# Products 2 and 4 of the query projection in a second level of Strassen's form, four query buffers and a new order of the cycle

## The chip, the cores and the metric

The kernel runs on one core of a Trainium2 chip. A core has TensorE (matmuls; results go to PSUM), VectorE, ScalarE and GpSimd (element-wise work) and SyncE, which here issues the DMAs. Each engine works through its own instruction queue in order, and waits on semaphores for the others. The metric is the device time of one execution in microseconds.

## The reference, cut to what matters

64 sequences of 128 tokens, 512 wide. All is in float32.

```python
def ref(x, attn_bias, mask, g_in, null_attn_bias, null_kv, Wq, Wkv, Wo, g_out):
    xn = layernorm(x, g_in)                       # (64, 128, 512)
    q = (xn @ Wq).reshape(b, n, 16, 64).transpose(0, 2, 1, 3) * 64 ** -0.5
    k, v = split(xn @ Wkv)                        # one head of 64 for all 16
    k, v = with_null_row(k, v, null_kv)
    sim = einsum('bhid,bjd->bhij', q, k) + bias   # bias: null column, attn_bias
    sim = where(causal and mask, sim, -max)
    out = einsum('bhij,bjd->bhid', softmax(sim), v)
    out = out.transpose(0, 2, 1, 3).reshape(b, n, 1024) @ Wo
    return x + layernorm(out, g_out)
```

## The kernel before

The sequences go in 16 groups `g` of four (`GB`). The 512 x 1024 query weight `wq` and a group's transposed tokens `xT[g]` (512 x 512) are cut into two by two blocks, and the query projection is one level of Strassen's form in Winograd's order: seven products instead of eight. `weight_sum` and `token_sum` make the sums (weights once, on VectorE; tokens four times per group, on GpSimd, tiles `xS`). `product` (L496) is, for one of four column blocks f, two matmuls with a stationary tile of 128 x 128 and 256 moving columns. Products 1, 6 and 7 gather in one PSUM tile `pa`, 5 and 3 in `pc`, product 2 is in `pw`; `keep` copies a state of `pa` on ScalarE, `q_out` adds it to another on VectorE and writes it into the query tile `qT`, which has two buffers of a whole group. The output projection has the same form for pairs of sequences (`out_product`, L758, `out_sum` on GpSimd).

The order of the steady part is written by hand, in `cycle(c)` for c = 1 to 29. A cycle carries two sequences through each stage: softmax of b0 = 2c and b1 = 2c+1 (`scores_max`, `exps`, `rinv`, `scale`, `blocks_T`), output projection of the pair from p = b0-2, norm and store of r = b0-4 and r+1, tokens of m = b0+10 and m+1 loaded and normalised, query products for f = 0, 1 (c even) or 2, 3 (c odd) of group (2c+4)//4, key and value products of sequences b0+6 and b0+7 (`key_values`: `kv_mm` L358 on TensorE, `kv_out` L373 on VectorE). It ends with `region(c)`: scores of sequences 2c+2 and 2c+3 (L551), then the values of b0 and b1 (L668).

Tokens are transposed on VectorE in blocks (`tokens_T`, L330) and go through memory: at the end of an even cycle `tokens_out` (L339) stores a finished group from `xb` to `xd`, next to `keys_send` (kb on VectorE L399, then kd L404) and `values_send` (L385). The odd cycle after it begins on SyncE with two loads of x (L127), four fetches of keys (L413), four of values (L391), a mask (L144) and the four fetches of `tokens_in` (L347), which fill `xT` of the group whose first sequence is b0+6. The stores of finished sequences (L839) and the loads for the residual (L137) follow in the same queue.

In `cycle` before, the key/value products come late: product 6 of the second half, then

```python
        key_values(b0 + 6)
        q_one(c, 7, 1)
        key_values(b0 + 7)
```

and after them `out_one(p, 3)`, products 3 and 4, `out_one(p, 4)` and `region(c)`. The token sums stand at the end of the odd cycles, behind `region`.

Of the kernel before, what the change touches and what calls it, by code (L numbers as in the profile page):

```python
# [17 lines left out]
def kernel(  # L18
# [63 lines left out]
    P = 128  # L82
# [347 lines left out]
    def q_tile(g):  # L430
        qT[g] = gp.tile([P, NF, GB, NQ, 2, Q], FP, tag="qT", name=f"qT_{g}")

    def q_part(g, c, lo=0, hi=GB):

        return qT[g][:, c % NF, lo:hi, :, c // NF, :]

    def q_half(c, h):
        if c == 0 and h == 0:
            q_tile(0)
        pq = (ps_y if h else ps_q).tile(  # L440
            [P, HT], FP, tag="XY"[c % 2] if h else "ac"[c % 2], name=f"pq_{c}_{h}"
        )
        two = slice(2 * h, 2 * h + 2)
        for kc in (2, 0, 3, 1):
# [8 lines left out]
            q_part(0, c, two.start, two.stop),  # L453
            pq.rearrange("p (t i q) -> p t i q", t=2, i=NQ),
        )

# [9 lines left out]
    def token_sum(g, k):  # L466
# [11 lines left out]
        nc.gpsimd.tensor_tensor(xS[g, k], p, m, ALU.subtract)  # L478

# [29 lines left out]
    def q_out(g, c, toks, tag, name=None):  # L509
        lo = toks.start // N  # L510
        o = q_part(g, c, lo, lo + 2)
# [33 lines left out]
    def heads(b, hf, to):  # L545
        g, t = divmod(b, GB)
        for f in range(NF):
            for r in range(2):
                rows = slice(r * DH, (r + 1) * DH)
                for i in range(2):  # L550
                    nc.tensor.matmul(  # L551
                        to[r][i * DH : (i + 1) * DH, f, :],
                        qT[g][rows, f, t, NQ - 1 - i if hf else i],
# [217 lines left out]
    def y_half(b, e):  # L771
        if b not in ys:
            if at_end:
                ys[b] = at_end[0][:, b - (B - 6)]
# [77 lines left out]
    def q_one(c, k, h):  # L852
# [82 lines left out]
    def cycle(c):  # L935
# [8 lines left out]
        if not first:  # L944
# [90 lines left out]
        if soft:  # L1035
            exps(b1, 1, 4, 7)
        out_one(p, 7)
        if soft:
            exps(b1, 1, 7)
# [369 lines left out]
```

## Time and profile before

| | |
|---|---|
| median of 3 runs | 1040.6 us (1040.02 to 1041.3) |
| the profiled execution | 1040.6 us |
| its span in the profile | 1038.8 us |
| mean granted TensorE clock | 0.998 |
| instructions | 31012 |

The profile lists for each engine its busy time, for groups of instructions their count and mean duration and the idle time before them with what ended it, the chain of work that ended last (followed back from the end, with the share of each engine), the same chain piece by piece in order of time, and the timeline of each engine. Times in a chain or timeline are start and duration in us from the span's start. A float32 matmul is recorded as two matmul records, so "x4" of a query product are two matmuls, and "x8" of a key/value product four. SPq is SyncE's queue: its rows are the issues of DMAs, not the transfers.

### The profile page before, as it was taken

What the parts mean: (1) busy time and instruction counts of PE and PEld (TensorE: products, weight loads), DVE (VectorE), ACT (ScalarE), POOL (GpSimd) and SP (SyncE); (2) the same over time, 40 slices, a digit from 0 to 9 for tenths busy, and PEclk for the clock granted to TensorE, in tenths of its full rate; (3) what the DMA queues carried; (4) which work ended last, traced back from release to release, by engine and by line L of the source; (5) the groups of instructions that cost most, each with busy time, mean ns of one, the idle gap of its engine ahead of it and who ended that gap; (6) DMA issues with size and microseconds to landing.
All of it is one profiled execution on the core that took longest, in us unless ns stands there. A gap on an engine that the chain in (4) does not pass through costs nothing.

```text
span 1038.8 us, 31012 instructions
## 1 busy us (share of the span) xinstructions
PE 1024.2 (99%) x11856; PEld 896.4 (86%) x11856; DVE 771.2 (74%) x1664; ACT 665.9 (64%) x2799; POOL 711.0 (68%) x530
## 2 busy tenths in 40 slices
PE   8999999999999999999999999999999999999996
PEld 7888888888888888888888888888888888888875
DVE  7776677787677786677776777776786876766688
ACT  2665677565776566776656776657765657765581
POOL 3697767676775857767577676757758587666774
PEclk9999999999999999999999999999999999999999
DMA  6633160432515134151341504334151341502202
GB/s 210 157 121 85 52 182 27 146 92 94 144 52 153 57 120 128 42 169 50 127 112 67 169 25 150 88 103 137 51 154 55 123 125 42 166 12 73 83 11 92
DMA packets 68690, 105.10 MB, mean 101 GB/s; under 512 B 8641, under 2 KB 32833, under 8 KB 66753
## 3 DMA queue, kind: packets, MB, share of 16 engines
q1 hardware_dynamic: 67440, 102.08, 32.3%
q8 instruction: 96, 1.57, 0.7%
q10 hardware_dynamic: 1104, 1.05, 0.3%
q14 instruction: 50, 0.40, 0.1%
HBM read 67.45 MB, written 35.65 MB: 99 GB/s over the span
## 4 chain that ended last, share of the span: by engine, by line
PE 92%; ACT 3%; DVE 3%; DMA 1%; POOL 1%; issue 1%; POOLq 0%; DVEq 0%; ACTq 0%
PE pa L496 20%; PE pyX L758 19%; PE pc L496 10%; PE pyY L758 9%; PE ps L551 9%; PE pkv L358 5%; PE pyw L758 5%; PE pw L496 5%; PE poX L668 4%; PE pq L445 2%; ACT s L599 2%; PE pos L668 2%; PE poY L668 1%; DMA x<-in_x_dram 1%; DVE y_end L821 1%
## 5 line engine op out<-in xcount | busy, mean ns | idle before, releaser
L599 ACT ACTIVATE s<-s,nmax 128x65 f32<-128x65 f32 (+1 forms) x1024 | 377.5, 393 | 0.0
L535 POOL TENSOR_TENSOR s<-biasp,mneg 128x1552 f32<-128x1552 f32 x64 | 206.2, 3223 | 70.6 <-DVE sb L635 58.9
L599 ACT ACTIVATION_READ_ACCUMULATOR s<-s,nmax 128x1 f32 x1024 | 221.3, 216 | 0.0
L620 POOL TENSOR_TENSOR s<-s,rinv 128x1024 f32<-128x1024 f32 (+1 forms) x128 | 190.4, 1488 | 44.5 <-DVE rinv L616 44.5
L635 DVE STREAM_TRANSPOSE sb<-s 128x1536 f32<-128x1536 f32 x64 | 113.5, 1773 | 43.2 <-POOL s L620 43.0
L585 DVE TENSOR_TENSOR s<-ps,s 128x256 f32<-128x256 f32 (+2 forms) x224 | 120.0, 605 | 16.9 <-PE ps L551 14.7
L496 PE MATMUL pa<-xS,wq 128*128 128x256 f32 x480 | 123.4, 379 | 0.5 <-ACT ku L507 0.5
L758 PE MATMUL pyX<-wo,oT 128*128 128x256 f32 x512 | 121.6, 380 | 0.3 <-POOL oT L741 0.3
L741 POOL TENSOR_TENSOR yS<-oT 128x512 f32<-128x512 f32 x32 | 40.9, 1278 | 117.2 <-ACT oT L708 113.0
L708 ACT ACTIVATE oT<-poX,nv 128x256 f32<-128x256 f32 x59 | 28.0, 475 | 143.8 <-PE poX L668 74.4
L590 DVE TENSOR_REDUCE nmax<-s 128x8 f32<-128x520 f32 (+1 forms) x128 | 116.4, 948 | 0.0
L758 PE MATMUL pyX<-wT,oT 128*128 128x256 f32 x488 | 115.4, 379 | 0.3 <-POOL oT L741 0.3
L758 PEld LDWEIGHTS pyX<-wo,oT 128*128 128x128 f32 x512 | 96.8, 190 | 15.3 <-issue 1.3
L758 PEld LDWEIGHTS pyX<-wT,oT 128*128 128x128 f32 x488 | 92.6, 190 | 13.3 <-POOL oT L741 0.7
L496 PEld LDWEIGHTS pa<-xS,wq 128*128 128x128 f32 x480 | 88.9, 190 | 11.7 <-ACT ku L507 0.9
L551 PEld LDWEIGHTS ps<-kT,qT 64*64 64x64 f32 x4096 | 85.6, 134 | 11.5 <-issue 11.4
L551 PE MATMUL ps<-kT,qT 64*64 64x128 f32 (+1 forms) x4096 | 93.7, 245 | 0.6 <-issue 0.6
L517 DVE TENSOR_TENSOR qT<-pc,ku 128x256 f32<-128x256 f32 x120 | 50.4, 420 | 58.6 <-ACT ku L507 43.5
L514 ACT COPY qT<-pa 128x256 f32<-128x256 f32 x60 | 23.0, 383 | 101.7 <-PE pa L496 101.7
L288 POOL TENSOR_TENSOR rstd<-rstd,nhalf 128x1 f32<-128x1 f32 x64 | 35.7, 559 | 66.6 <-DVE rstd L287 66.6
L668 PE MATMUL pos<-sb,vr 32*64 32x128 f32 (+1 forms) x1792 | 81.0, 321 | 0.0
L668 PE MATMUL poY<-sb,vr 32*64 32x128 f32 x720 | 74.4, 347 | 0.0
(113 smaller groups left out, 2299.8 us busy)
## 6 DMA issues: line engine op xcount, KB each, us to landing
x<-in_x_dram SPq DMA_DIRECT2D x64, 256.0 KB, 5.4
res<-in_x_dram SPq DMA_DIRECT2D x64, 256.0 KB, 3.1
out_dram<-y SPq DMA_DIRECT2D x58, 256.0 KB, 2.0
xd<-xb SPq DMA_DIRECT2D x14, 1024.0 KB
xT<-xd SPq DMA_DIRECT2D x56, 256.0 KB, 6.1
vr<-vd SPq DMA_DIRECT2D x64, 128.0 KB, 8.5
kT<-kd SPq DMA_DIRECT2D x64, 64.0 KB, 9.6
kd<-kb SPq DMA_DIRECT2D x16, 128.0 KB
```

Of the source, the lines that this page charges most:

```text
L358: nc.tensor.matmul(pkv, xT[g][:, t, kc, :], wkv[:, kc, :], start=(kc == 0), stop=(kc == KC - 1),)
L496: nc.tensor.matmul(prod[tag], w[:, kc, f * P : (f + 1) * P], t[:, :, kc, :], start=(start and kc == 0), stop=(kc == HK - 1), skip_group_ch ...
L517: nc.vector.tensor_tensor(o, p, k, ALU.add)
L535: nc.gpsimd.tensor_tensor(S[b], biasp, mneg[:, t].unsqueeze(1).broadcast_to([P, R8, ROW]), ALU.add,)
L551: nc.tensor.matmul(to[r][i * DH : (i + 1) * DH, f, :], qT[g][rows, f, t, NQ - 1 - i if hf else i], kT[g][rows, 0 : NQ if hf else NQ // 2, ...
L585: nc.vector.tensor_tensor(sv, ps, sv, ALU.add)
L590: nc.vector.tensor_reduce(nmax[b][:, hf], S[b][:, :, WITH_NULL[hf]], AX.X, ALU.max, negate=True)
L599: nc.scalar.activation(row, row, AF.Exp, bias=nmax[b][:, hf, k : k + 1], accum_out=rsum[b][:, hf, k : k + 1],)
L620: nc.gpsimd.tensor_tensor(sv, sv, rinvs.pop((b, hf)).unsqueeze(2).broadcast_to([P, R8, sv.shape[2]]), ALU.mult,)
L635: nc.vector.transpose(sb.rearrange("p j e q -> p e j q"), S[b][:, :, 1 : ROW - 1].rearrange("p e (j k) -> p e j k", k=Q),)
L668: nc.tensor.matmul(po[s][rows, half], vr[g][quad(s), j, t, :], sb[quad(s), slots, r * NF : (r + 1) * NF, :], start=start, stop=True, skip_ ...
L758: nc.tensor.matmul(prod[key], h[:, c, :], w[:, c, :], start=(start and c == 0), stop=(c == HC - 1), skip_group_check=not start,)
```

## The change

Products 2 (weight block a12) and 4 (a22) get a second level from c = 2 on. Each is cut again into two by two blocks of 128 rows, 128 columns and 128 tokens, for a pair of f at once: `leaf(c, k, stage)` issues seven matmuls of 128 columns in four stages (one, three, two, one), all into three slices of one PSUM tile of `ps_w`, and after each stage VectorE adds slices onto the query tile (`onto`, two additions in stage 1, else one). `leaf_weights` makes the sums of weight blocks on GpSimd, three of them at the end of cycle 1 for each product and one at the start of cycle 2; `leaf_sums` makes those of the tokens, four for each product and group, in even cycles. Where product 2 was added to a kept copy of product 1, product 1 is now copied into the query tile (`first_into`) and the narrow products are added to it there; product 4 is added to a copy of the state behind product 7.

The query tile becomes four tiles by pair of f and pair of sequences, one buffer each, whose places change between even and odd groups; the tile for the last six outputs becomes three tiles in the same places.

The order of `cycle` is new for all cycles: the second half's product 1 and `key_values(b0 + 6)` come before `out_one(p, 6)`, `key_values(b0 + 7)` comes last before `region`, both `bias_add` stand behind the last `scale`, and the token sums stand at the start of the even cycles. The diff, without changes of indices that follow from the tiles and without `q_first`, which nothing calls:

```diff
@@ -427,19 +427,27 @@
     s3 = a21
     xS, prod, kept = {}, {}, {}
-    def q_tile(g):
-        qT[g] = gp.tile([P, NF, GB, NQ, 2, Q], FP, tag="qT", name=f"qT_{g}")
-    def q_part(g, c, lo=0, hi=GB):
-        return qT[g][:, c % NF, lo:hi, :, c // NF, :]
-    def q_half(c, h):
+    GH, FH = GB // 2, NF // 2
+    def q_tile(g, fp):
+        for h in range(2):
+            slot = 2 * fp + h if g % 2 == 0 else fp + 2 * h
+            qT[g, fp, h] = gp.tile(
+                [P, FH, GH, NQ, 2, Q], FP, tag=f"q{slot}", name=f"qT_{g}_{fp}_{h}", bufs=1
+            )
+    def q_part(g, c, h):
+        f = c % NF
+        return qT[g, f // FH, h][:, f % FH, :, :, c // NF, :]
...
             4: (b21, xS.get((g, 2))),
         }[k]
         nc.gpsimd.tensor_tensor(xS[g, k], p, m, ALU.subtract)
+    LEAF = 2
+    wL = const.tile([P, 2, 3, FH, P], FP, name="wL")
+    xL, leaves = {}, {}
+    def by_block(tag):
+        return prod[tag].rearrange("p (t i q) -> p t i q", t=2, i=NQ)
+    def first_into(g, c, h):
+        nc.scalar.copy(q_part(g, c, h), by_block("a"))
+    def leaf_blocks(k):
+        w = (a12 if k == 2 else a22).rearrange("p k (f r m) -> p k r f m", r=2, m=P)
+        return w[:, 0, 0], w[:, 1, 0], w[:, 0, 1], w[:, 1, 1]
+    def leaf_weights(k, j):
+        w11, w12, w21, w22 = leaf_blocks(k)
+        t1, t2, t4 = (wL[:, k // 4, i] for i in range(3))
+        o, p, m, op = {
+            1: (t1, w21, w22, ALU.add),
+            2: (t2, t1, w11, ALU.subtract),
+            4: (t4, w12, t2, ALU.subtract),
+            3: (w21, w11, w21, ALU.subtract),
+        }[j]
+        nc.gpsimd.tensor_tensor(o, p, m, op)
+    def leaf_tokens(g, k):
+        b = xT[g][:, 0:GH, hi_k] if k == 2 else xS[g, 4]
+        return b[:, 0, 0], b[:, 1, 0], b[:, 0, 1], b[:, 1, 1]
+    def leaf_sums(g, k):
+        xL[g, k] = gp.tile([P, 3, N], FP, tag=f"xL{k}", name=f"xL{k}_{g}", bufs=1)
+        b11, b12, b21, b22 = leaf_tokens(g, k)
+        t1, t2, t3 = (xL[g, k][:, i] for i in range(3))
+        for o, p, m in ((t1, b12, b11), (t3, b22, b12), (t2, b22, t1), (b12, b21, t2)):
+            nc.gpsimd.tensor_tensor(o, p, m, ALU.subtract)
+    def leaf(c, k, stage):
+        g, f = divmod(2 * c + 4, GB)
+        if g >= NG:
+            return
+        fp = f // FH
+        if stage == 0:
+            leaves[k] = ps_w.tile([P, 3, N], FP, tag="w", name=f"pl{k}_{g}_{f}")
+        pw, pY, pX = (leaves[k][:, i] for i in range(3))
+        w11, w12, w21, w22 = (w[:, fp] for w in leaf_blocks(k))
+        v1, v2, v4 = (wL[:, k // 4, i, fp] for i in range(3))
+        b11, t4, b21, b22 = leaf_tokens(g, k)
+        t1, t2, t3 = (xL[g, k][:, i] for i in range(3))
+        out = qT[g, fp, 0][:, :, :, :, k // 4, :]
+        def mm(to, w, t, start=False):
+            nc.tensor.matmul(to, w, t, start=start, stop=True, skip_group_check=True)
+        def onto(o, p):
+            nc.vector.tensor_tensor(o, p, o, ALU.add)
+        def one(p):
+            return p.rearrange("p (i q) -> p i q", i=NQ)
+        def two(p):
+            return p.rearrange("p a (i q) -> p a i q", i=NQ)
+        if stage == 0:
+            mm(pX, w11, b11, True)
+            onto(out[:, 0, 0], one(pX))
+        elif stage == 1:
+            mm(pw, w12, b21)
+            mm(pX, v2, t2)
+            mm(pY, v1, t1)
+            onto(out[:, 0], two(leaves[k][:, 0:3:2]))
+            onto(out[:, 1, 1], one(pY))
+        elif stage == 2:
+            mm(pX, w21, t3)
+            mm(pY, v4, b22)
+            onto(out[:, :, 1], two(leaves[k][:, 1:3]))
+        else:
+            mm(pX, w22, t4)
+            onto(out[:, 1, 0], one(pX))
...
@@ -854,11 +970,14 @@
         g, f = divmod(i, GB)
         if g >= NG:
             return
-        if k == 1 and f == 0:
-            q_tile(g)
+        if k == 1 and f % FH == 0:
+            q_tile(g, f // FH)
         if k == 1:
             product(g, f, 1, ps_q, "a")
-            keep("a", "p1")
+            if c >= LEAF:
+                first_into(g, f, 0)
+            else:
+                keep("a", "p1")
         elif k == 2:
             product(g, f, 2, ps_w, "w")
             q_out(g, f, lo_t, "w", "p1")
@@ -869,8 +988,14 @@
             keep("a", "u2")
         elif k == 7:
             product(g, f, 7, ps_q, "a", start=False)
-            keep("a", "u3")
-            q_out(g, HC + f, hi_t, "c", "u3")
+            if c >= LEAF:
+                first_into(g, HC + f, 0)
+                nc.vector.tensor_tensor(
+                    q_part(g, HC + f, 1), by_block("c"), q_part(g, HC + f, 0), ALU.add
+                )
+            else:
+                keep("a", "u3")
+                q_out(g, HC + f, hi_t, "c", "u3")
...
@@ -950,116 +1075,163 @@
                 load_mask(kg + 1)
             if (m - 2) // GB < NG:
                 tokens_in((m - 2) // GB)
+        if c == LEAF:
+            for k in (2, 4):
+                leaf_weights(k, 3)
+        if soft:
+            scores_max(b1, 0)
+        if pair:
+            values_out(p, (0, 2))
+            values_out(p, (1, 3))
         if soft:
             scores_max(b0, 0)
-            scores_max(b0, 1)
-            scores_max(b1, 0)
-        if c % 2 and n0 < B:
-            mask_neg(n0 // GB)
-            if n1 == B - 3:
-                bias_add(B - 2)
+        if first and LEAF <= c and 2 * c + 4 < B:
+            token_sum(c // 2 + 1, 1)
+            token_sum(c // 2 + 1, 2)
+            token_sum(c // 2 + 1, 3)
+        q_one(c, 1, 0)
+        if first and LEAF <= c and 2 * c + 4 < B:
+            token_sum(c // 2 + 1, 4)
+        if fin:
+            pair_stats(r)
+        if first and LEAF <= c and 2 * c + 4 < B:
+            leaf_sums(c // 2 + 1, 2)
         if pair:
-            values_out(p, (0, 2))
             values_out(p + 1, (0, 2))
-        q_one(c, 1, 0)
-        if pair:
-            values_out(p, (1, 3))
             values_out(p + 1, (1, 3))
-            out_sum(p, 0)
-        q_one(c, 2, 0)
+        if soft:
+            exps(b0, 0, 0, 2)
+        if c < LEAF:
+            q_one(c, 2, 0)
+        if fin:
+            pair_stats(r + 1)
+        q_one(c, 5, 0)
         if soft:
             scores_max(b1, 1)
-        q_one(c, 5, 0)
+        if c >= LEAF:
+            leaf(c, 2, 0)
+        q_one(c, 6, 0)
         if soft:
-            exps(b0, 0, 0, 2)
-        q_one(c, 6, 0)
-        if fin:
-            for b in (r, r + 1):
-                pair_stats(b)
-                pair_pow(b)
-        if soft:
-            exps(b0, 0, 2, 7)
+            exps(b0, 0, 2, 8)
+            scores_max(b0, 1)
+        if first and LEAF <= c and 2 * c + 4 < B:
+            leaf_sums(c // 2 + 1, 4)
+        if pair:
+            out_sum(p, 0)
         out_one(p, 1)
+        q_one(c, 7, 0)
+        out_one(p, 2)
         if pair:
             out_sum(p, 1)
         if soft:
-            exps(b0, 0, 7)
+            exps(b0, 1, 0, 6)
+        if fin:
+            pair_pow(r)
+        if soft:
             rinv(b0, 0)
             scale(b0, 0)
-        q_one(c, 7, 0)
-        if pair:
-            out_sum(p, 2)
-        if soft:
-            exps(b0, 1, 0, 6)
-        out_one(p, 2)
-        if pair:
-            out_sum(p, 3)
-        q_one(c, 3, 0)
-        if soft:
-            exps(b0, 1, 6)
-            rinv(b0, 1)
-            scale(b0, 1)
-        q_one(c, 4, 0)
-        if fin:
-            for b in (r, r + 1):
-                pair_nmr(b)
-                pair_norm(b)
-            pair_gain(r)
-            pair_residual(r)
-            store(r)
-        out_one(p, 6)
         if toks:
             norm_stats(m)
             norm_stats(m + 1)
+        if c < LEAF:
+            q_one(c, 4, 0)
+        if pair:
+            out_sum(p, 3)
+        if fin:
+            pair_pow(r + 1)
+        if soft:
+            exps(b0, 1, 6, 8)
+        q_one(c, 3, 0)
+        if soft:
+            rinv(b0, 1)
+        if fin:
+            pair_nmr(r)
+        q_one(c, 1, 1)
+        if c >= LEAF:
+            leaf(c, 2, 1)
+        if fin:
+            pair_norm(r)
+        key_values(b0 + 6)
+        if c % 2 and n0 < B:
+            mask_neg(n0 // GB)
+        if fin:
+            pair_gain(r)
+            pair_residual(r)
         if soft:
             exps(b1, 0, 0, 6)
-            blocks_T(b0)
+            exps(b1, 0, 6, 8)
+            rinv(b1, 0)
+        out_one(p, 6)
+        if fin:
+            pair_nmr(r + 1)
+        if c < LEAF:
+            q_one(c, 2, 1)
+        if pair:
+            out_sum(p, 2)
+        if fin:
+            store(r)
+            pair_norm(r + 1)
+            pair_gain(r + 1)
+        if c >= LEAF:
+            leaf(c, 4, 0)
+            leaf(c, 2, 2)
+        if soft:
+            scale(b0, 1)
+            exps(b1, 1, 0, 4)
+        q_one(c, 6, 1)
+        if n1 == B - 3:
+            bias_add(B - 2)
+        q_one(c, 5, 1)
         out_one(p, 5)
         if soft:
-            exps(b1, 0, 6)
-            rinv(b1, 0)
+            exps(b1, 1, 4, 8)
+        if toks:
+            norm_apply(m)
+        if soft:
+            blocks_T(b0)
             scale(b1, 0)
-        if nxt:
-            bias_add(n0)
+            rinv(b1, 1)
         if fin:
-            pair_gain(r + 1)
             pair_residual(r + 1)
+        out_one(p, 7)
+        q_one(c, 7, 1)
+        if fin:
             store(r + 1)
+        if c >= LEAF:
+            leaf(c, 4, 1)
+        if soft:
+            scale(b1, 1)
+        if c >= LEAF:
+            leaf(c, 2, 3)
+        out_one(p, 4)
         if pair:
             load_res(p)
             load_res(p + 1)
-        q_one(c, 1, 1)
-        if soft:
-            exps(b1, 1, 0, 4)
-        q_one(c, 2, 1)
-        if soft:
-            exps(b1, 1, 4, 7)
-        out_one(p, 7)
-        if soft:
-            exps(b1, 1, 7)
-            rinv(b1, 1)
-            scale(b1, 1)
-        q_one(c, 5, 1)
-        q_one(c, 6, 1)
-        if toks:
-            norm_apply(m)
-            norm_apply(m + 1)
-        key_values(b0 + 6)
-        q_one(c, 7, 1)
-        key_values(b0 + 7)
         if soft:
             blocks_T(b1)
+        if toks:
+            norm_apply(m + 1)
         if nxt:
+            bias_add(n0)
             bias_add(n1)
-        out_one(p, 3)
+        if c >= LEAF:
+            leaf(c, 4, 2)
         q_one(c, 3, 1)
         if toks:
             tokens_T(m)
             tokens_T(m + 1)
-        q_one(c, 4, 1)
+        out_one(p, 3)
+        if c < LEAF:
+            q_one(c, 4, 1)
+        if c >= LEAF:
+            leaf(c, 4, 3)
         if soft:
-            nc.tensor.addr_align(256, offset=183 if c == B // 2 - 3 else 223)
-        out_one(p, 4)
+            nc.tensor.addr_align(256, offset=205 if c == B // 2 - 3 else 223)
+        key_values(b0 + 7)
+        if c == 1:
+            for k in (2, 4):
+                for j in (1, 2, 4):
+                    leaf_weights(k, j)
         if first:
             kg = (b0 + 7) // GB
             if kg < NG:
@@ -1068,9 +1240,7 @@
             if toks:
                 tokens_out(m // GB)
         region(c)
-        if c % 2 and (2 * c + 6) // GB < NG:
-            for k in range(1, 5):
-                token_sum((2 * c + 6) // GB, k)
...
@@ -1225,7 +1395,7 @@
     region(0)
     for c in range(1, B // 2 - 2):
         cycle(c)
-    at_end.append(gp.tile([P, 8, DIM], FP, tag="qT", name="y_end"))
+    at_end.append({})
```

More of the change, by code (lines that the diff above doesn't have):

```diff
@@ L428, with q_half @@
     xS, prod, kept = {}, {}, {}
-    def q_tile(g):
-        qT[g] = gp.tile([P, NF, GB, NQ, 2, Q], FP, tag="qT", name=f"qT_{g}")
-    def q_part(g, c, lo=0, hi=GB):
-        return qT[g][:, c % NF, lo:hi, :, c // NF, :]
-    def q_half(c, h):
+    GH, FH = GB // 2, NF // 2
[8 more added lines that the diff above has]
+        return qT[g, f // FH, h][:, f % FH, :, :, c // NF, :]
+    def q_half(c, h, at=None):
         if c == 0 and h == 0:
[L439 to L442, printed above, removed]
+            for fp in range(2):
+                q_tile(0, fp)
+        tag = at or ("XY"[c % 2] if h else "ac"[c % 2])
+        pq = (ps_q if tag in "ac" else ps_y).tile([P, HT], FP, tag=tag, name=f"pq_{c}_{h}")
         two = slice(2 * h, 2 * h + 2)
@@ L452, in q_half, with q_first @@
         nc.scalar.copy(
-            q_part(0, c, two.start, two.stop),
+            q_part(0, c, h),
             pq.rearrange("p (t i q) -> p t i q", t=2, i=NQ),
         )
+    def q_first(f, k, tag):
+        pool = {"a": ps_q, "c": ps_q, "X": ps_y, "Y": ps_y, "s": ps_s, "w": ps_w}[tag]
+        if f == 0 and k == 1:
+            for fp in range(2):
+                q_tile(0, fp)
+        product(0, f, k, pool, tag, start=k in (1, 2, 5))
+        o = {
+            1: (f, 0),
+            2: (f, 0),
+            6: (f, 1),
+            7: (HC + f, 1),
+            4: (HC + f, 0),
+            5: (HC + f, 1),
+            3: (f, 1),
+        }[k]
+        o = q_part(0, *o)
+        if k in (2, 3, 5):
+            nc.vector.tensor_tensor(o, by_block(tag), o, ALU.add)
+        else:
+            nc.scalar.copy(o, by_block(tag))
     def weight_sum(k):
@@ L509, in q_out @@
     def q_out(g, c, toks, tag, name=None):
-        lo = toks.start // N
-        o = q_part(g, c, lo, lo + 2)
+        o = q_part(g, c, toks.start // HT)
         p = prod[tag].rearrange("p (t i q) -> p t i q", t=2, i=NQ)
@@ L552, in heads @@
                         to[r][i * DH : (i + 1) * DH, f, :],
-                        qT[g][rows, f, t, NQ - 1 - i if hf else i],
+                        qT[g, f // FH, t // GH][
+                            rows, f % FH, t % GH, NQ - 1 - i if hf else i
+                        ],
                         kT[g][rows, 0 : NQ if hf else NQ // 2, t, :],
@@ L773, in y_half @@
             if at_end:
-                ys[b] = at_end[0][:, b - (B - 6)]
+                k = (b - (B - 6)) // 2
+                if k not in at_end[0]:
+                    at_end[0][k] = gp.tile([P, 2, DIM], FP, tag=f"q{k}", name=f"y_end_{k}", bufs=1)
+                ys[b] = at_end[0][k][:, b % 2]
             else:
```

1 line of the change is left out of this document (added).

## The prediction

> **What bounds the kernel now.** I began with the page: shares of each engine, granted clock, chain of work that ended last.
>
> ```profile
> PE 1024.2 (99%) x11856; PEld 896.4 (86%) x11856; DVE 771.2 (74%) x1664; ACT 665.9 (64%) x2799; POOL 711.0 (68%) x530
> PEclk9999999999999999999999999999999999999999
> PE 92%; ACT 3%; DVE 3%; DMA 1%; POOL 1%; issue 1%; POOLq 0%; DVEq 0%; ACTq 0%
> ```
>
> TensorE sets the time: it is on 92% of the chain, at full clock throughout. Any time in which it waits is added to the end, and any matmul time removed is taken off. So I read next the chain inside one cycle of the steady part, from one group of score products (`ps`, the start of `region`) to the next. It is an odd cycle, c = 13.
>
> ```profile
> 504.70 2.84 PE ps L551 x128
> ...
> 510.00 1.06 PE pa L496 x4
> 511.06 0.86 PE pw L496 x4
> ...
> 513.65 1.73 PE pyX L758 x8
> ...
> 528.32 0.89 PE pkv L358 x8
> ...
> 536.15 2.84 PE ps L551 x128
> ```
>
> A cycle is 536.15 - 504.70 = 31.45 us, all of it matmuls. One query product is 0.86 (two matmuls of 256 columns, so 0.43 each), one output product 1.73, one key/value product 0.89 (four matmuls of 128 columns, 0.2225 each). The first query product of a cycle starts 5.30 after the scores, and this cycle's first key/value product 23.62 after them. That product is the first reader of a token group (`xT`) which SyncE fetches in this very cycle; in even cycles the group is there already. SyncE's queue:
>
> ```profile
> 506.72 0.46 SPq L339 DMA_DIRECT2D xd<-xb  x1
> 507.22 1.92 SPq L127 DMA_DIRECT2D x<-in_x_dram  x2
> 511.47 7.79 SPq L391 DMA_DIRECT2D vr<-vd  x4
> 519.84 1.80 SPq L347 DMA_DIRECT2D xT<-xd  x4
> 523.36 5.49 SPq L839 DMA_DIRECT2D out_dram<-y  x2
> ...
> DMA to landing us min/median/max: 4.8/6.1/7.2
> SPq L391 <- DMA x<-in_x_dram: 64.1, 26, 3.0
> ```
>
> The first five rows are in order of time; the sixth is from the view of the tile xT, the seventh from that of SyncE's waits. The tokens go out to memory (`xd`) 2.0 us after the scores began, and the four fetches back (`xT`) are issued only from 519.84, because the fetches of values ahead of them wait for loads of x (64.1 us in 26 waits). The last of the four starts near 519.84 + 1.80 - 0.43 = 521.2 and with the median of 6.1 lands at 527.3, which is 22.6 after the scores. The traffic says the same:
>
> ```profile
> 525.00:527.00 2.00, 2.00 (x11) 1.77 (x10) 1.97 (x4) 2.00 (x12) 0.56 (x1) 1.00 0.91 221
> 527.00:528.20 1.20, 1.20 (x8) 1.04 (x7) 1.17 (x4) 1.20 (x7) 1.01 (x2) 1.00 0.06 21
> ```
>
> The last two columns are the busy share of the DMA engines and GB/s: 221 until 527, 21 after. So the key/value product at 528.32 stands about 1 us behind its data. In another odd cycle even that was too little:
>
> ```profile
> 252.77 2.84 PE ps L551 x128
> ...
> 276.39 0.09 issue
> 276.48 1.13 PE pkv L358 x8
> ...
> 284.55 2.84 PE ps L551 x128
> ```
>
> The product takes 1.13 there instead of 0.89, and the cycle 31.78 instead of 31.45. The fetch is already as late as TensorE can bear.
>
> **The narrow products.** Per cycle from c = 2 on, products 2 and 4 of one f pair, 2 x 4 matmuls of 0.43 = 3.46, become 2 x 7 of 128 columns. The key/value product is the nearest row: same shapes, a new stationary tile for each matmul, 0.2225. 14 x 0.2225 = 3.115. Saved: 0.345 a cycle, over 28 cycles (2 to 29) **-9.7 us**. Bounds: the weight loads are recorded longer than their spacing,
>
> ```profile
> L358 PEld LDWEIGHTS pkv<-wkv,xT 128*128 128x128 f32 x512 | 66.5, 191 | 3.9 <-issue 0.9
> L373 DVE TENSOR_TENSOR kvt<-pkv,nkv 128x128 f32<-128x128 f32 x64 | 18.0, 282 | 3.5 <-PE pkv L358 3.4
> L517 DVE TENSOR_TENSOR qT<-pw,kp 128x256 f32<-128x256 f32 x60 | 25.0, 417 | 2.3 <-PE pw L496 0.3
> L478 POOL TENSOR_TENSOR xS<-xT 128x512 f32<-128x512 f32 x30 | 38.4, 1280 | 0.0
> L727 POOL TENSOR_TENSOR wT<-wo,wT 128x1024 f32<-128x1024 f32 x2 | 4.9, 2437 | 0.1
> sum 31.50, PE 31.50 PEld 27.71 DVE 23.92 ACT 21.00 POOL 19.44; mean PE 3.94 PEld 3.46 DVE 2.99 ACT 2.62 POOL 2.43
> 511.51 0.39 ACT L507 COPY kp<-pa 128x256 f32<-128x256 f32 x1
> ```
>
> and if the two loads of 191 of each narrow matmul did not overlap, it would cost 0.382 and the edit +62 us. They overlap in the key/value products, so I keep 0.2225.
>
> **What VectorE, ScalarE and GpSimd gain.** VectorE gets six additions of 128 columns (0.28) and four of 256 (0.42) per cycle for two of 0.42: +2.5 us. ScalarE loses two copies. GpSimd gets eight differences of 128 columns in every even cycle; by the rows of 512 and 1024 columns one costs 0.12 + 128 x 0.00226 = 0.41, so +3.3. The sum row above is that of an odd cycle: VectorE 23.9 of 31.5, then 26.4 of 31.1; GpSimd in an even one 19.4, the four sums xS (5.1) and 3.3, that is 27.8. I cost this at nothing, since TensorE's work covers it. Tightest is the first copy `first_into` of a cycle: it has the place in ScalarE's queue that the row of kp has, which ends at 511.90, and product 6, which now follows products 1, 5 and a narrow one, could start at 510.00 + 1.06 + 0.86 + 0.22 = 512.14. In odd cycles the last narrow addition, right ahead of the scores, has a few tenths as well. If such a cover is gone, 0.5 us a cycle is 14 us; that is the upper end.
>
> **The four query buffers** take the halves of the old ones in the order in which the scores give them up, and the writes follow the scores on the same cycle boundary as before: nothing, with no row that says otherwise. The end buffers take them after the last cycle.
>
> **The new order: the key/value product moves.** This is the term that decides. In the changed program it is issued behind products 1, 5, a narrow one, 6, output 1, 7, output 2, 3, the next product 1 and three narrow ones: 1.06 + 0.86 + 0.22 + 0.86 + 1.73 + 0.86 + 1.73 + 0.86 + 0.86 + 0.67 = 9.71 after the first query product, **15.0 after the scores** instead of 23.6. SyncE's queue ahead of the fetch is unchanged: kd, vd, xd, two of x, four of kT, four of vr, the mask. So TensorE waits there, in program order, and all its later matmuls with it (output 6, the rest of the narrow ones, six query products, the next scores); behind VectorE's addition `kvt` stand the gain and residual of an output and rinv, for which GpSimd's scaling waits, and ScalarE waits for output 6.
>
> When will it land? Its chain starts with kb on VectorE,
>
> ```profile
> 505.45 0.40 DVE L399 STREAM_TRANSPOSE kb<-kvt 128x256 f32<-128x256 f32 x1
> ```
>
> 1.15 after the scores. The new order puts the cycle's second key/value product right ahead of the scores; its addition (0.28) and kb (0.40) then end about 0.85 after: 0.3 earlier. The store at 523.36 shared the DMA engines with the fetch (one more 256 KB beside 1024 KB at 221 GB/s, 1.2 us at most); now it comes after the wait, for which I take 0.6. So 22.6 - 0.3 - 0.6 - 15.0 = **6.7 us of wait per odd cycle**, bounds by the shortest landing, 4.8: 5.2, and by the longest, 7.2, without the 0.6: 8.4. Twelve cycles (3 to 25) have this form: 80.4. The first and the last differ:
>
> ```profile
> 64.06 2.84 PE ps L551 x128
> 77.41 2.12 SPq L347 DMA_DIRECT2D xT<-xd  x4
> ...
> 882.30 2.84 PE ps L551 x128
> 892.58 1.82 SPq L347 DMA_DIRECT2D xT<-xd  x4
> ```
>
> c = 1: last issue near 79.1, landing 85.2, 21.1 after the scores; the product stands at 15.84 there (eight wide query products ahead and two output products): 5.3. c = 27, where no x is loaded any more: landing 17.75, less 0.3, less 15.0: 2.4. Together **+88.1**.
>
> **What the wait does to the clock.** Rows from the two ends of the program (the window's length, then busy time of each engine, clock last but two):
>
> ```profile
> 1.30:4.60 3.30, 3.24 (x15) 3.24 (x16) 0.26 (x2) 0.00 (x0) 0.34 (x5) 1.00 0.61 135
> 4.60:6.30 1.70, 1.68 (x15) 1.49 (x14) 1.54 (x4) 1.49 (x2) 0.56 (x1) 1.00 1.02 341
> ...
> 1030.40:1035.40 5.00, 0.00 (x0) 0.00 (x0) 4.01 (x9) 0.00 (x0) 1.97 (x2) 1.00 0.23 88
> 1035.40:1038.80 3.40, 0.00 (x0) 0.00 (x0) 0.42 (x1) 0.00 (x0) 0.00 (x0) 0.50 0.20 77
> ```
>
> After its last matmul TensorE keeps clock 1.00 for 5 us, then 0.50. At the start the same small matmuls run 15 in 3.3 us, then 15 in 1.7: half speed for the first 3.3 us. A wait of 6.7 is longer than 5, so I expect half speed for 3.3 us of work after each, a loss of 1.65: 12 x 1.65 = **+19.8**. Bounds: nothing, and twice that. [...]
>
> **Once, at c = 2.** Eight weight sums of 256 columns (0.70 each by the rows above, 5.6) are queued on GpSimd ahead of that cycle's token sums.
>
> ```profile
> 538.34 1.30 POOL L478 TENSOR_TENSOR xS<-xT 128x512 f32<-128x512 f32 x1
> 541.45 1.06 PE pa L496 x4
> ```
>
> The first token sum is ready 1.81 before the first query product; product 5, its reader, now comes 1.06 after that: 5.6 - 1.81 - 1.06 = **+2.7** (bounds 1 and 5).
>
> **Sum**: 88.1 + 19.8 - 9.7 + 2.7 = +100.9 on the profiled span of 1038.8 gives 1139.7. That execution took 1040.6, 1.8 more, and is the median of the three runs: forecast **1141 us**.
>
> **Rivals.** (a) The wait, but the clock is kept or soon back: 1141 - 20 = 1121. For it: nothing here shows a gap of several us inside the program. Against: the 5 us at the end. (b) Wait and clock as above, and VectorE or ScalarE late besides by 0.5 a cycle, or a longer recovery: about 1160. For it: the margin of 0.24; against: where TensorE waits, the others catch up. (c) Narrow products at the rate of unoverlapped weight loads, +62: 1203. The change would not do what it says; the key/value rows speak against it. (d) The other side: the fetch is not late. Place: SyncE's queue in odd cycles; it decides from a landing before 15.0 + 0.7 after the scores, where the waits (14 x 0.7) eat the saving. Then 1040.6 - 9.7 + 2.7 = 1033.6. For it: the waits of vr on x are a matter of queueing, which may fall out otherwise. Against: even c = 27, without loads of x, lands at 17.75.
>
> **How the numbers follow.** Forecast 0.68, (a) 0.17, (b) 0.07, (c) 0.03, (d) 0.05. The forecast's own range, from 12 waits of 5.2 to 8.4, is 1123 to 1161. Taking in (a) at its shorter waits (1121 - 18) and (b) at its longer ones, the range is 1100 to 1175. Within 0.2% (2.1 us, about what a measurement of this kernel tells from no change) is only the edge of (d), 0.01; faster 0.04; slower 0.95.
>
> **What would show it.** In the changed profile odd cycles are some 39 to 40 us from scores to scores and even ones 31.1; `pkv` carries idle time ended by the DMA of xT, about 6 us in 12 cycles; the slices of the clock show values under 9; narrow matmuls are 0.22 apart. A gap of `pkv` under 1 us, or cycles of 31.1 throughout, makes the prediction wrong; longer even cycles would make (b) right.

## The result, and the profile after

The changed kernel takes **1164.28 us** (median of 4 runs, 1162.82 to 1165.41) against 1040.95 of the kernel before (4 runs, 1040.02 to 1041.47): ratio 1.1185, 95% interval 1.1166 to 1.1204. The profiled span is 1161.4 us, 122.6 more than before; the mean granted clock is 0.957.

The page of the changed kernel: engine shares, and the slices of TensorE and of its clock.

```profile
PE 1051.6 (91%) x12192; PEld 925.7 (80%) x12192; DVE 822.5 (71%) x1888; ACT 652.0 (56%) x2743; POOL 763.4 (66%) x650
PE   8989979799797997979979799797997979999996
PEclk9999989999899998989989899898998989999999
```

TensorE fell from 99% to 91%, in a pattern that comes back every second cycle, and the clock has slices of 8. The waits of TensorE name the place (engine, line, waited for: us in total, times, longest):

```profile
PE pkv L358 <- DMA xT<-xd: 93.7, 14, 8.1
PEld pc L608 <- DVE qT L993: 7.6, 27, 0.3
```

14 waits of the key/value product for the token fetch make 93.7 of the 122.6. The second row comes up below. One odd cycle of the new kernel, scores at 497.44 (c = 13 counted from `region`; the cycle at 504.70 that the prediction called c = 13 is c = 15 by that count, and has the same form): TensorE, then SyncE's queue, then the time from issue to landing of all 56 fetches of xT in the run.

```profile
512.23 0.61 PE L564 MATMUL pl<-xL,wL 128*128 128x128 f32 x4
520.15 2.04 PE L358 MATMUL pkv<-wkv,xT 128*128 128x128 f32 x8 [7.32 <-DMA xT<-xd]
```
```profile
498.35 0.33 SPq L404 DMA_DIRECT2D kd<-kb  x1
...
504.76 7.02 SPq L391 DMA_DIRECT2D vr<-vd  x4
...
512.36 1.80 SPq L347 DMA_DIRECT2D xT<-xd  x4
524.42 5.84 SPq L955 DMA_DIRECT2D out_dram<-y  x2
```
```profile
DMA to landing us min/median/max: 4.7/6.2/6.4
```

TensorE is through with the narrow products 15.4 after the scores (512.84); SyncE issues the fetch only from 14.9 after them, and the product starts 22.7 after them. The clock in the same cycle (window, its length, busy time of each engine, clock, DMA share, GB/s):

```profile
497.44:512.80 15.36, 15.36 (x289) 13.27 (x288) 12.80 (x30) 9.86 (x45) 5.80 (x6) 1.00 0.55 168
512.80:516.50 3.70, 0.04 (x1) 0.00 (x0) 1.06 (x6) 3.28 (x17) 3.61 (x5) 1.00 0.83 208
516.50:520.20 3.70, 0.04 (x1) 0.07 (x1) 0.00 (x0) 0.41 (x3) 1.77 (x1) 0.51 0.54 114
520.20:523.40 3.20, 3.20 (x12) 2.93 (x13) 1.16 (x4) 0.00 (x0) 0.00 (x0) 0.51 0.00 0
523.40:538.00 14.60, 14.60 (x86) 13.11 (x84) 10.88 (x24) 7.08 (x24) 9.51 (x5) 1.00 0.28 93
```

3.7 us into the wait the clock goes to half, and stays there for the first 3.2 us of work: the key/value product, 1.06 in the next fence, takes 2.04. From 520.20 to 523.40 ScalarE, GpSimd and the DMA engines stand still, so TensorE is on the path. From scores to scores the cycle takes 537.98 - 497.44 = 40.54 us.

An even cycle (c = 14), where the fetch is there, from TensorE's timeline:

```profile
537.98 2.91 PE L662 MATMUL ps<-kT,qT 64*64 64x128 f32 x128
...
545.10 0.38 PE L564 MATMUL pl<-xT,wq 128*128 128x128 f32 x2
545.45 1.10 PE L608 MATMUL pa<-xS,wS 128*128 128x256 f32 x4
546.39 1.89 PE L871 MATMUL pyX<-wo,oT 128*128 128x256 f32 x8
...
550.71 1.13 PE L608 MATMUL pc<-xT,wS 128*128 128x256 f32 x4
551.68 1.03 PE L608 MATMUL pa<-xT,wq 128*128 128x256 f32 x4
...
553.21 1.06 PE L358 MATMUL pkv<-wkv,xT 128*128 128x128 f32 x8
...
555.83 0.39 PE L564 MATMUL pl<-xS,wq 128*128 128x128 f32 x2
556.05 0.39 PE L564 MATMUL pl<-xL,wq 128*128 128x128 f32 x2
556.28 0.39 PE L564 MATMUL pl<-xT,wL 128*128 128x128 f32 x2
```

The last three rows show narrow matmuls 0.22 apart, as priced. Yet the even cycles take 31.44, not 31.1. Product 6 starts 0.35 behind a narrow matmul of 0.22 and takes 0.94 to the next start instead of 0.86: 0.2 lost behind `first_into`. Product 3, which waits for the addition behind product 7 (the row of L993 above), takes 0.97 instead of 0.86: 0.1. So about 0.3 of the 0.345 comes back as waits in every cycle.

**The account.** The 14 odd cycles are together 121.8 us longer than 14 times 31.45. Of this 93.7 is the wait; the other 28.1 is mainly the clock: 2.9 to 3.0 in two cycles, 0.2 in c = 27 whose wait is 1.65, 1.6 to 2.7 in the other eleven. By the clock's own steps TensorE worked 51.5 us at half speed behind these waits, and half of that is 25.8. c = 2 is 1.6 longer, the last cycle 0.8 shorter: 122.6.

### The profile page after: what moved, and what is told of

Read it like the earlier page. It is cut to its first block, busy times and chain, and to the rows that moved or that the text cites. A ratio compares the mean times of both kernels' runs of the same rounds, so it can differ in the third digit from the quotient of the medians.

```text
span 1161.4 us, 31470 instructions
## 1 busy us (share of the span) xinstructions
PE 1051.6 (91%) x12192; PEld 925.7 (80%) x12192; DVE 822.5 (71%) x1888; ACT 652.0 (56%) x2743; POOL 763.4 (66%) x650
## 5 line engine op out<-in xcount | busy, mean ns | idle before, releaser
L712 ACT ACTIVATION_READ_ACCUMULATOR s<-s,nmax 128x1 f32 x1024 | 217.2, 212 | 0.0
L358 PE MATMUL pkv<-wkv,xT 128*128 128x128 f32 x512 | 80.1, 308 | 93.7 <-DMA xT<-xd 93.7
L358 PEld LDWEIGHTS pkv<-wkv,xT 128*128 128x128 f32 x512 | 73.0, 219 | 96.4 <-issue 94.3
L871 PE MATMUL pyX<-wT,oT 128*128 128x256 f32 x488 | 129.1, 412 | 0.5 <-POOL oT L854 0.3
L703 DVE TENSOR_REDUCE nmax<-s 128x8 f32<-128x520 f32 (+1 forms) x128 | 118.8, 948 | 0.0
L871 PEld LDWEIGHTS pyX<-wT,oT 128*128 128x128 f32 x488 | 98.7, 213 | 14.1 <-POOL oT L854 0.7
L373 DVE TENSOR_TENSOR kvt<-pkv,nkv 128x128 f32<-128x128 f32 x64 | 18.4, 288 | 124.6 <-PE pkv L358 124.6
L904 ACT COPY kyu<-pyX 128x256 f32<-128x256 f32 x62 | 22.5, 363 | 123.8 <-PE pyX L871 120.2
L567 DVE TENSOR_TENSOR qT<-pl,qT 128x128 f32<-128x128 f32 (+1 forms) x280 | 84.0, 333 | 0.0
```

The costliest lines, as they stand in the source:

```text
L358: nc.tensor.matmul(pkv, xT[g][:, t, kc, :], wkv[:, kc, :], start=(kc == 0), stop=(kc == KC - 1),)
L567: nc.vector.tensor_tensor(o, p, o, ALU.add)
L703: nc.vector.tensor_reduce(nmax[b][:, hf], S[b][:, :, WITH_NULL[hf]], AX.X, ALU.max, negate=True)
L712: nc.scalar.activation(row, row, AF.Exp, bias=nmax[b][:, hf, k : k + 1], accum_out=rsum[b][:, hf, k : k + 1],)
L871: nc.tensor.matmul(prod[key], h[:, c, :], w[:, c, :], start=(start and c == 0), stop=(c == HC - 1), skip_group_check=not start,)
```

## The experiments

My theory: the place of `key_values(b0 + 6)` alone makes the loss, by a wait for the fetch and the clock that it costs. Rivals: the narrow products or the additions on VectorE and ScalarE make part of it; the lateness is only SyncE's order; the long cycles are not the clock's.

### The place of the product

**`e4_before_kv_early`**: the kernel before, with nothing but that place changed.

```diff
         q_one(c, 4, 0)
+        key_values(b0 + 6)
...
         q_one(c, 6, 1)
-        key_values(b0 + 6)
         q_one(c, 7, 1)
```

> The kernel before with one line moved: key_values(b0 + 6) stands behind q_one(c, 4, 0), 9.7 us after the first query product and 15.0 us after the scores, as in the changed kernel. Theory (the place of this product alone decides): waits of about 7 us in the odd cycles, half speed behind them, 1163 us (1145 to 1175). Rival (the wait needs the narrow products or the rest of the new order): within 10 us of before, 1041 to 1051.

Measured 1203.3, ratio 1.1554 (1.1538 to 1.157). Its waits:

```profile
PE pkv L358 <- DMA xT<-xd: 105.4, 13, 9.0
PEld pa L496 <- ACT ku L507: 25.1, 29, 0.9
PE pa L496 <- ACT ku L507: 13.4, 29, 0.5
```

One moved line is enough for the whole loss, and more: in the twelve cycles from 3 to 25 the waits are 7.8 to 9.0, the mean granted clock of the run is 0.943, where the changed kernel has 0.957, and in every cycle product 7 stands directly behind product 6 now and waits for ScalarE's copy `ku`. This last wait is not one of the fetch: even cycles take 32.18 instead of 31.45, some 21 us in all. The size was missed; the direction holds.

**`e1_kv_late`**: the changed kernel, the product moved behind the last narrow matmuls.

```diff
             leaf(c, 2, 1)
...
-        key_values(b0 + 6)
...
             leaf(c, 2, 3)
+        key_values(b0 + 6)
         out_one(p, 4)
```

> The changed kernel with one line moved: key_values(b0 + 6) stands behind leaf(c, 2, 3), ahead of out_one(p, 4), about 25 us after the scores. Theory (the wait for xT and the clock lost in it are all that made the change slower): odd cycles fall from some 40.5 to 31.4 us like the even ones, no DMA wait of pkv, clock 1.00 throughout, 1042 us (1039 to 1045). Rival (the new order makes the other engines late, and the fetch only hides it): odd cycles stay several us longer than even ones, the time stays above 1060.

Measured 1109.84, ratio 1.066 (1.0645 to 1.0674): missed by 68. No wait for the fetch is left, but another is in its place:

```profile
PE pkv L358 <- DVE qT L567: 47.9, 27, 2.0
```
```profile
188.40:190.40 2.00, 0.15 (x2) 0.06 (x1) 1.70 (x6) 0.64 (x3) 2.00 (x2) 1.00 0.39 142
190.40:193.80 3.40, 3.40 (x13) 3.04 (x14) 1.67 (x2) 0.00 (x0) 2.82 (x1) 0.55 0.41 148
```

The key/value product takes the PSUM place of a narrow product that VectorE still has to read, 1.8 us on average, in every cycle. The second fence (windows around the wait of an even cycle) shows that such a wait, 1.85 here, can cost the clock too: 0.55 in the mean of the next 3.40 us. It doesn't in every cycle: the mean granted clock of the run is 0.985, in the kernel before 0.998, so an estimated 29 us went at half clock (0.013 x 2 x 1108.7), eight or nine such stretches for 27 waits.

**`e1b_kv_after_out4`**: the same one output product later, so that VectorE has time.

```diff
             leaf(c, 2, 1)
...
-        key_values(b0 + 6)
...
             bias_add(n1)
+        key_values(b0 + 6)
         if c >= LEAF:
             leaf(c, 4, 2)
```

> The changed kernel with key_values(b0 + 6) moved behind out_one(p, 4), ahead of leaf(c, 4, 2), where the PSUM place it takes over from the first narrow product has been read. Theory (the late fetch is all; the 1.8 us of wait per cycle in e1_kv_late was that place, not yet read by VectorE): no wait of pkv, clock 1.00, all cycles 31.4 to 31.5 us but c = 2, 1042 us (1039 to 1045). Rival (the other engines are too late for the new order): a wait of over 1 us per cycle stays, 1070 us or more.

Measured 1055.28, ratio 1.014 (1.0125 to 1.0155); the wait for the fetch and the lost clock are gone (mean granted 0.998), and with them 109 of the 123 us, by one moved line. What is left, 32.0 us a cycle:

```profile
PE pyX L871 <- ACT kyu L904: 7.4, 25, 0.5
```

Output product 4 waits for ScalarE's copy behind output product 7. With the key/value product behind it TensorE is there 0.9 sooner, ScalarE is not. By the cycles (31.96 and 32.02 less 31.44) it costs 0.52 to 0.58.

**`e5_kv_late_one_level`**: `e1_kv_late` without the second level and its sums.

```diff
-    LEAF = 2
+    LEAF = 99
...
-            leaf_sums(c // 2 + 1, 2)
...
-            leaf_sums(c // 2 + 1, 4)
...
-        if c == 1:
-            for k in (2, 4):
-                for j in (1, 2, 4):
-                    leaf_weights(k, j)
```

> As the first of this set (key/value product late, new order), but without the second level in any cycle: products 2 and 4 stay whole, no leaf_sums and no leaf_weights. Theory (narrow products run at the key/value product's 0.2225 us): 0.34 us a cycle slower than with the second level, and without the loss of cycle 2: 1042 + 9.7 - 1.6 = 1050 us (1047 to 1053). Rival (the second level saves nothing, its waits give it back): within 2 us of the first of this set.

1048.21, ratio 1.0067 (1.0053 to 1.0081), cycles of 31.76: the expected size. It has no narrow product, so it lacks the PSUM wait of `e1_kv_late` and can't be compared with it for the worth of the second level.

### Why the fetch is late

**`e9_fetch_first`**: the changed kernel, the fetch moved ahead of those of keys and values in SyncE's queue (the instruction offset of the scores in TensorE's program follows).

```diff
             load_x(b)
...
+            if (m - 2) // GB < NG:
+                tokens_in((m - 2) // GB)
...
-            if (m - 2) // GB < NG:
-                tokens_in((m - 2) // GB)
```

> The changed kernel with the key/value product left at its early place, and tokens_in moved in SyncE's queue ahead of the fetches of keys and values, right behind the two loads of x. Theory (the fetch is late by the queue ahead of it: xd is written some 7 us after the scores, then the four fetches could be issued by 9 and land by 15): the wait shrinks from 7.2 us to under 1, the clock stays 1.00, 1043 us (1041 to 1058). Rival (the transfers themselves set the landing, the queue only shows it): waits of over 4 us stay, 1100 us or more.

Measured 1118.77, ratio 1.0741 (1.0722 to 1.076): a good third of the loss is back, not all. SyncE's timeline with scores at 474.23, its wait ahead of the fetch, the landing:

```profile
476.53 1.94 SPq L127 DMA_DIRECT2D x<-in_x_dram  x2
482.07 1.75 SPq L347 DMA_DIRECT2D xT<-xd  x4
483.87 4.90 SPq L413 DMA_DIRECT2D kT<-kd  x4
```
```profile
SPq L347 <- DMA xd<-xb: 43.2, 14, 4.3
```
```profile
DMA to landing us min/median/max: 5.1/9.0/11.6
```

The fetch is now issued 7.8 after the scores instead of 14.9, held by its own store xd, 3.1 us on average. But from issue to landing it takes 9.0 in the median instead of 6.2, with loads of x ahead of it and eight fetches of keys and values behind it. The waits are 2.7 to 5.2, and they still cost clock: its mean is 0.976, an estimated 49 us at half (0.022 x 2 x 1112.9). The queue was about half of the lateness; the transfers are the rest. That the other transfers stretch it is argued from the order, not isolated.

### The clock

**`e3_fill_wait`**: 24 matmuls of an identity, of 128 columns, ahead of the key/value product in odd cycles, written into its own tile, which the product then starts anew.

```diff
-    def kv_mm(m, pkv=None):
+    def kv_mm(m, pkv=None, busy=0):
...
+        for _ in range(busy):
+            nc.tensor.matmul(pkv, ident, ident, start=True, stop=True)
...
-        key_values(b0 + 6)
+        key_values(b0 + 6, 24 if c % 2 else 0)
```

> The changed kernel with 24 matmuls of 128 columns put ahead of the first key/value product in odd cycles, into its own PSUM tile (their results are overwritten): 5.3 us of work in place of waiting. Theory (a wait of over 5 us costs half speed behind it): the clock stays 1.00, the odd cycles lose some 1.8 us each, c = 27 gains 3.7: 1144 us (1138 to 1150). Rival (TensorE's speed behind the wait does not matter, since the others bound it there): odd cycles stay as they are, 1164 to 1168 us.

1311.51, ratio 1.2603. It says nothing on the clock: the scores are aligned to 256 instructions, so the added ones brought 160 filling instructions in each odd cycle, and TensorE idles on them:

```profile
PE pkv L360 <- issue: 134.3, 15, 9.6
```

**`e3b_fill_wait_aligned`**: the same, with the offset of that alignment following the added instructions.

> As e3_fill_wait, but the instruction alignment at the cycle's end follows the 96 added instructions, so that no filling instructions are put there (in e3_fill_wait they took 9.6 us in each odd cycle). Theory (a wait of over 5 us costs half speed behind it): clock 1.00 throughout, odd cycles some 1.8 us shorter than in the changed kernel, c = 27 longer by 3.7: 1143 us (1138 to 1150). Rival (the half speed costs nothing): 1164 us or more.

Measured 1163.35, ratio 1.1171 (1.1141 to 1.1202). By the total, the rival is right that nothing is gained; by the cycle it is not. Cycle c = 13 with the scores at 495.67:

```profile
511.70:517.20 5.50, 5.50 (x50) 5.34 (x48) 1.19 (x6) 3.81 (x19) 5.28 (x5) 1.00 0.86 198
517.20:518.40 1.20, 0.08 (x2) 0.08 (x1) 0.00 (x0) 0.00 (x0) 0.11 (x1) 1.00 0.01 3
518.40:534.60 16.20, 16.20 (x92) 14.66 (x92) 12.06 (x27) 7.18 (x24) 9.26 (x4) 1.00 0.25 83
```

The wait is filled but for 1.1 us, the clock stays at 1.00, and from the key/value product to the next scores it takes 16.2 us; in the changed kernel (520.15 to 537.98) 17.8. So this stretch of low clock costs 1.6 us. The rest of the gain was lost: the fill took the whole wait, the shifted alignment added 0.2 to 0.8 in `region` of most cycles, and the waits for the fetch that remain (23.8 us in 12, the longest 3.2) still cost clock: its mean is 0.990, not 0.998.

### What the second level is worth without the wait

**`e2_two_waits`**: `e1b_kv_after_out4`, and two edits against the two small waits of each cycle: `values_out(p, (3,))` goes behind product 1, so that `first_into` comes sooner in ScalarE's queue, and the second half's product 1 goes between products 7 and 3.

```diff
-            values_out(p, (1, 3))
+            values_out(p, (1,))
...
         q_one(c, 1, 0)
+        if pair:
+            values_out(p, (3,))
...
+        q_one(c, 1, 1)
         q_one(c, 3, 0)
...
-        q_one(c, 1, 1)
```

> e1b_kv_after_out4 with two more changes of order: one of the four values_out ahead of first_into goes behind it, and q_one(c, 1, 1) goes ahead of q_one(c, 3, 0). Theory (the narrow products do save 0.34 us a cycle, and the waits of product 6 for first_into, 0.20, and of product 3 for VectorE, 0.10, give it back): cycles of 31.15 us, 0.3 x 28 = 8.4 less than e1b_kv_after_out4: 1033 us (1031 to 1036). Rival (narrow products save nothing): as e1b_kv_after_out4, within 2 us.

1050.51, ratio 1.0094 (1.0079 to 1.0109). Both waits are gone, and the one at output product 4 grows in their place:

```profile
PE pyX L871 <- ACT kyu L904: 10.8, 25, 0.5
```

Cycles are 31.83; c = 27 and 28, where no tokens are normalised, 31.19 and 31.21. ScalarE's queue there holds `norm_apply(m)`.

**`e6_weights_early`**: `e2_two_waits`, with the six `leaf_weights` of cycle 1 moved into the middle of it, behind `scale(b0, 0)`.

```diff
             scale(b0, 0)
+        if c == 1:
+            for k in (2, 4):
+                for j in (1, 2, 4):
+                    leaf_weights(k, j)
...
-        if c == 1:
-            for k in (2, 4):
-                for j in (1, 2, 4):
-                    leaf_weights(k, j)
```

> e2_two_waits with six of the eight leaf_weights moved from the end of cycle 1 into its middle, behind scale(b0, 0). Theory (they are what makes product 5 of cycle 2 wait, 0.8 us, and an output product 0.2): cycle 2 as long as the others, 1.0 to 1.6 us less than e2_two_waits. Rival (cycle 2 is late for another reason, or cycle 1 gets the wait): no gain, within 0.5 us.

1050.14, ratio 1.0093, against 1.0094: c = 2 is 0.9 shorter, c = 1 0.8 longer. The sums cost the same in either of the two places.

**`e7_norm_later`**: `e2_two_waits`, with `norm_apply(m)` behind output product 7.

```diff
-        if toks:
-            norm_apply(m)
...
         q_one(c, 7, 1)
...
+        if toks:
+            norm_apply(m)
```

> e2_two_waits with norm_apply(m) behind q_one(c, 7, 1) instead of ahead of the copy behind output product 7. Theory (in e1b_kv_after_out4 and e2_two_waits output product 4 waits 0.6 us a cycle for that copy, which ScalarE reaches only after norm_apply): cycles of 31.2 us, 1034 us (1032 to 1038). Rival (ScalarE is late by more than one instruction): a wait of 0.3 us or more stays, 1042 us or more.

1041.73 against 1040.74, ratio 1.001 (1.0002 to 1.0019): within 0.2% of the kernel before, span 1039.6, clock 0.998. The wait at output product 4 is gone, and the cycles take 31.45. TensorE's timeline and the load's wait behind it:

```profile
498.73 0.39 PE L564 MATMUL pl<-xT,wq 128*128 128x128 f32 x2
498.95 1.89 PE L871 MATMUL pyX<-wT,oT 128*128 128x256 f32 x8
500.90 1.16 PE L358 MATMUL pkv<-wkv,xT 128*128 128x128 f32 x8
```
```profile
PEld pkv L358 <- DVE qT L567: 11.9, 27, 0.5
```

The output product takes 1.95 to the next start instead of 1.73, and the key/value product 0.99 instead of 0.89: 0.3 for VectorE's reading of the narrow product's PSUM place. All narrow products are in, the key/value product is late again, and 122 of the 123 us are gone. No version beat the kernel before.

**`e10_fetch_first_two_waits`**: the diff of `e9_fetch_first` and the two order edits of `e2_two_waits` together, the key/value product in its early place.

> e9_fetch_first with the two changes of order of e2_two_waits (values_out split around first_into, product 1 of the second half ahead of product 3). Theory (0.20 of product 6 and 0.10 of product 3 given back per cycle): 8 us less than e9_fetch_first, cycles of 31.15 us, faster than before: 1035 us (1032 to 1040). Rival (another wait takes their place, as ScalarE's did in e2_two_waits): less than 4 us gained.

1120.87, ratio 1.0777: no gain over `e9_fetch_first` in the whole. In the odd cycles from 3 to 25 the key/value product is ready 0.3 sooner, but its fetch lets it start only 20.0 after the scores in the mean instead of 19.2, so it waits longer; why the fetch comes later was not looked into. The even cycles, where no fetch is waited for, answer what the expectation asked. Two score groups in a row of TensorE's timeline:

```profile
518.49 2.91 PE L662 MATMUL ps<-kT,qT 64*64 64x128 f32 x128
549.61 2.91 PE L662 MATMUL ps<-kT,qT 64*64 64x128 f32 x128
```

All steady even cycles take 31.12, without a wait of TensorE in them: 0.32 less than in the changed kernel and 0.33 less than in the kernel before, where 0.345 was priced. So the narrow products do save what they should, once product 6 and product 3 no longer wait.

**`e11_fetch_first_one_level`**: this, with the edits of `e5_kv_late_one_level` to `LEAF` and the sums.

> e10_fetch_first_two_waits without the second level: products 2 and 4 whole in all cycles, no leaf_sums, no leaf_weights. Theory (14 narrow matmuls at 0.2225 us for 8 wide ones at 0.43): 0.34 us a cycle more than e10, less the late cycle 2: 7 to 10 us slower than e10_fetch_first_two_waits. Rival (second level worth nothing on the chip): within 2 us of it.

1139.86, ratio 1.0963 (1.0909 to 1.1017). The 19 us more don't measure the second level: even cycles take 32.85, with waits that the other has not (0.64 at a product 1, 0.23 at an output product). What the second level is worth against whole products in the same order was not isolated, and no run had both the fetch in time and cycles of 31.12.

## Why the prediction was right

The forecast was 1141, the time 1164.28; the mechanism held, its sizes were 23 short. Its errors did not cancel: of the 21.7 that are missing on the span, 8.3 are the clock, some 9 the narrow products and 5.6 the wait, less 1.1 at c = 2.

- **The wait for the fetch**: 88.1 predicted, 93.7 measured, 7.2 in the mean of the twelve cycles for 6.7, 5.25 for 5.3 at c = 1, 1.65 for 2.4 at c = 27. TensorE comes 15.4 after the scores, not 15.0, by the small waits ahead of it. kd did go out 0.33 earlier and the store did come after the wait, but the landing stayed at 22.6 in the mean: the deductions of 0.3 and 0.6 were wrong. The fetch was issued 14.9 after the scores, where it had been 15.1, and the two deductions brought nothing. The prediction's lower bound of the wait, 5.2, comes to 5.4 by its own rows (a landing 4.8 after 521.2); only the low end of the range, 1123, rests on it.
- **The place as cause**: shown from both sides by one moved line each, `e4_before_kv_early` and `e1b_kv_after_out4`; `e7_norm_later` brings back the rest. Rival (d) is out: no odd cycle had its fetch in time.
- **The clock**: 19.8 predicted, some 28.1 measured. The step that failed is "A wait of 6.7 is longer than 5, so I expect half speed for 3.3 us of work": the 5 us at the end of the program did not hold inside it. The drop came 3.2 to 4.7 us into the wait, and c = 1, whose wait of 5.25 the prediction did not charge, paid 2.4 too. Half clock lasted 6.83 us (10.24 in two cycles), of which the part in the wait costs nothing; the work behind it was 3.0 to 5.7 us in the twelve cycles, 3.9 in the mean instead of 3.3. Half of their work at half clock is 23.3. What sets the moment of the drop was not shown.
- **The narrow products**: priced right, 0.22 each, but the -9.7 came to nothing in steady cycles of the changed kernel. The step that failed is "I cost this at nothing, since TensorE's work covers it": the margin of 0.24 at `first_into` was not enough, and the addition behind product 7, which I did not look at, holds product 3. Rival (b), 1160, came nearest in time, by the longer recovery it allowed and by this lateness, at 0.3 a cycle instead of 0.5. By the prediction's own sign, longer even cycles, (b) is right in part. With the key/value product late, in `e2_two_waits` and `e7_norm_later`, only c = 27 and 28 reach 31.2; with it early, in `e10_fetch_first_two_waits`, all steady even cycles take 31.12, so the price was right and the cover was wrong.
- **c = 2**: 2.7 predicted, 1.6 measured. Rivals (a) and (c) are out: the clock did drop (0.957 in the mean), and the weight loads do overlap (0.19 each as recorded, two to a narrow matmul of 0.22).

## What to carry to other kernels

Before moving a product on the engine that sets the end, look for what it reads first and when that lands, counted from the same mark in the cycle; here a product with 1 us of slack was moved 8.6 us ahead. Count the clock with the wait: here it added 30% to the price of the waits. And when a saving of 0.3 a cycle is spread over reordered short products, look at each reader of a PSUM place and each copy that stands between two of them: here they took it all. Behind the late key/value product each that was mended showed the next; in the order of the changed kernel mending two gave the saving back.

## What the runs showed of the hardware

- In the changed kernel half clock lasted 6.83 us behind eleven of the 13 waits of 5.25 to 8.14 us, and 10.24 behind two (c = 3 and 19). It began 3.2 to 4.7 us into the wait.
- A wait of 1.65 us in the changed kernel (c = 27) lost no clock: 1.00 in it and in the 10 us behind it. One of 1.85 in `e1_kv_late` did, 0.55 in the next 3.40 us, and by that run's estimate most of its 27 waits, at most 2.0 long, did not. What sets them apart was not shown.
- 160 filling instructions (256 less the 96 added) in TensorE's program took 9.6 us in `e3_fill_wait`.
- Product 3 of the changed kernel (c = 14), whose weight load waits for VectorE (0.3 at most), takes 0.97 to the next start; product 1 behind it takes 0.86.
